# Output weights multiplied into the values, a last softmax by halves, and a new order of folding, in a four-layer kernel on one Trainium2 core

## The chip, the cores and the metric

One core of one Trainium2 chip runs the whole program. The metric is device time in microseconds (us). Runs of one kernel are compared by their fast state. Time before the change: 3512.23 us, the median of 3 runs (3511.39 to 3512.83).

## The reference, cut to what matters

The network has four layers. The change is in layer 0, a deformable attention over 2 samples of 512 channels and 32x32 pixels with 8 heads. Heads are handled two at a time, so there are 8 "pairs" (4 of each sample), with 1024 queries and 64 keys per head. What is costly is not the attention but its position bias: a small network with 128 hidden units runs for each query and key.

```
off  = tanh(pointwise(gelu(depthwise(q)))) * 4        # where the keys are sampled
kv   = grid_sample(xn, grid + off)
k, v = kw @ kv, vw @ kv                               # per head
pos  = grid_q[:, None] - grid_kv[None, :]
bias = relu(relu(signlog(pos) @ cpb_w1 + b1) @ cpb_w2 + b2) @ cpb_w3 + b3
attn = softmax(q k^T / 8 + bias)
out  = out_w @ concat_heads(attn @ v) + out_b         # <- the order of these two products changes
x    = x + out ;  x = x + mlp(bn2(x))
```

Some weights of layer 2 are multiplied together once, early in layer 0 ("folding"); its result does not depend on the data.

## The kernel before

The bias of all 8 pairs takes 256 steps of four points each. VectorE writes a point's first hidden layer, `h1`, into a ring of buffers; TensorE (PE) multiplies it (`z`), ScalarE applies the relu (`h`), VectorE and small DMA transfers join the parts of two steps ("joins"), and every 8 steps `third` multiplies the joined parts into the scores `sim`. The work for the next pair and the softmax of the last one run "behind", a piece per half step.

```python
ring = [one.tile([P, HW], F32, name=f"h1{k}") for k in range(4)]            # 4 buffers of its own
ring += [qkv2...[:, k * HW : (k + 1) * HW] for k in range(6)]               # 8 that lie where later
ring += [proj2...[:, k * HW : (k + 1) * HW] for k in range(2)]              # the MLP weights go (wa)
...
AHEAD = 8                                                                   # h1 is written 8 points ahead
for i in range(steps + 2):
    if i == steps:
        (w1s,) = load_w(wa, "wa", [a["mlp_w1"]])                            # 4 MB
        pps.append(zt([P, HW], "pp"))
        project_out(pps[0], 1, range(NPAIR - 2), oTs[B - 1])
    for k, part in enumerate((1, 0, 3, 2)):
        p = 4 * i + AHEAD + k
        if p < 4 * steps:
            h1s[p] = first(p)                                               # ring[p % len(ring)]
        if i < steps:
            parts.setdefault(i, {})[part] = second(i, four, part)           # z, then relu
        ...
        if i >= 3 and i % 2 and k == 0 and i < steps:
            nc.sync.dma_start(out=joins[i - 3][1:P:2], in_=joins[i - 2][0:P:2])
        if i >= 3 and i % 2 and k == 3 and i < steps:
            nc.gpsimd.dma_start(out=joins[i - 3][1:P:2], in_=joins.pop(i - 2)[1:P:2], accum_op=ALU.add)
        ...
```

The end of a pair, before (cut to the last pair's path):

```python
simb = two.tile(...); nc.scalar.activation(simb, sim, AF.Identity, bias=simbias[t])
pt = zt([P, 8, P], "pt")                        # 8 transposes of simb
nc.vector.tensor_reduce(mx, ptv, ..., ALU.max)  # then 16 exponentials, sums, division
pa = pt if last else zt([P, 8, P], "pa")        # 8 transposes back
nc.scalar.copy(aT, pa...)
pv = ...
for half in range(2):
    nc.tensor.matmul(pv[:, n], vbd[t], aT[:, n], start=True, stop=True)     # values
    if last:
        nc.scalar.copy(oT[:, pr, n], pv[:, n])
...
project_out(pp, m, ...)                         # 4 blocks: out_w on oT of the 4 pairs, then added to x
```

`zt` hands out in turn three buffers of 1024 columns in PSUM, to which this kernel's products are written and which `z`, `pt`, `pp`, `pb` and the rest share.

## Time and profile before

| stretch (us from the start) | what | length | PE busy |
|---|---|---|---|
| 0 to 62 | loads, offsets of pair 0, folding | 62 | 56.6 |
| 62 to 2009 | 256 bias steps | 1947 | 1940.8 |
| 2009 to 2063 | end of the last pair (the tail) | 54 | 42.9 |
| 2063 to 3510 | MLP and layers 1 to 3, untouched | 1447 | |

In this trace the granted clock is 0.50 or 0.51 in four stretches of the first 2063 us: for 3.4 us from 10.9 and from 2038.4, for 6.8 us from 38.2 and from 2018.0. 3.4 us of half clock are called a window below, so the longer stretches are two each; what starts one is not shown. In PE's rows, `128*32` (as for `z`) and `128*128` tell two forms of product apart; the prediction calls the form a mode. From the issue of the 4 MB load at 2004.77 to 2018.80 the DMA moved 299 GB/s.

The prediction further on shows the rows this table is cut from. Two more views of the kernel before are used later. The first is the chain of waits in the folding (start, length, what ran): small products `po`, `row` and `pb` (here the kernel's tile `pb2`, not the `pb` of the loop, which comes up later) stand together, and the folding's own products `pf` after them.

```profile
36.26 0.38 PE po L371 x2
36.64 1.00 PE row L715 x8
37.64 2.56 PE pb L135 x16
40.20 6.02 PE pf L135 x8
```

The second is the timeline of DMA issues just before the last `z` ends at 2009.39:

```profile
2004.77 2.31 SPq L119 DMA_DIRECT2D wa<-in_mlp_w  x4
2005.56 0.86 POOL L784 DMA_DIRECT2D h<-h  x1 [5.73 <-DVE h L543]
2007.04 0.83 POOL L780 DMA_DIRECT2D h<-h  x1 [0.61 <-DMA h<-h]
```

The 4 MB load of the MLP weights (`wa`) is issued 2.3 us ahead of the last join, the POOL line at 2007.04. Which edit of the change alters that order turns out to be the question of this study.

### The profile page before, as it was taken

How to read it: one execution, taken by the hardware profiler on the slowest of the kernel's cores; microseconds unless marked ns; L12 is line 12 of the kernel's file. 1: busy time of each engine (PE TensorE's matmuls, PEld its weight loads, DVE VectorE, ACT ScalarE, POOL GpSimd, SP SyncE). 2: the span in 40 equal slices, each digit the busy share in tenths (PEclk: the TensorE clock that was granted, in tenths of full speed). 3: DMA queues.
4: the chain of work that ended last, by engine and by line, in shares of the span. 5: the costliest groups of instructions: out<-in, count | busy, mean ns of one | idle time of the engine just before them, and what ended most of it. 6: DMA issues, size and time to landing. Idle time of an engine off the chain costs nothing.

```text
span 3510.3 us, 58708 instructions
## 1 busy us (share of the span) xinstructions
PE 3470.8 (99%) x24269; PEld 1452.0 (41%) x24269; DVE 2474.9 (71%) x2724; ACT 1761.3 (50%) x2478; POOL 494.2 (14%) x581
## 2 busy tenths in 40 slices
PE   9999999999999999999999999999999999999999
PEld 4333333333333333333333269999433333444443
DVE  6999999999996999999999835455264374130223
ACT  4867867867864868768776611112243242111110
POOL 0222222222221222222222200000001000000000
PEclk9999999999999999999999999999999999999999
DMA  5776676666674676666766710001100000000000
GB/s 171 149 150 145 130 152 142 143 146 136 145 150 88 144 149 134 142 145 136 149 144 145 163 64 12 13 10 57 35 1 1 1 0 0 15 0 0 6 30 25
DMA packets 133683, 313.38 MB, mean 89 GB/s; under 512 B 21088, under 2 KB 66528, under 8 KB 132640
## 3 DMA queue, kind: packets, MB, share of 16 engines
q0 software_dynamic: 57040, 200.31, 30.7%
q1 hardware_dynamic: 76224, 108.71, 9.1%
q8 instruction: 193, 3.16, 0.4%
q14 instruction: 82, 0.67, 0.1%
q10 hardware_dynamic: 144, 0.52, 0.0%
HBM read 64.12 MB, written 10.75 MB: 21 GB/s over the span
## 4 chain that ended last, share of the span: by engine, by line
PE 90%; DVE 6%; ACT 2%; issue 2%; DVEq 0%; POOL 0%; ACTq 0%; POOLq 0%
PE z L529 43%; PE pw L135 6%; PE pm L1266 5%; PE pma L135 5%; PE pmv L135 5%; PE pmb L135 4%; PE score L1377 4%; PE score L135 3%; PE pv L1425 3%; DVE wa L512 2%; PE sim L556 2%; DVE h L543 2%; PE ppr L1297 2%; PE pmp L135 2%; PE pp L637 1%
## 5 line engine op out<-in xcount | busy, mean ns | idle before, releaser
L538 ACT ACTIVATE h<-z,b2h 128x1024 f32<-128x1024 f32 x1024 | 1134.8, 1115 | 520.1 <-PE z L529 504.7
L529 PE MATMUL z<-wa,cpb_w 128*32 128x512 f32 x10880 | 1196.6, 593 | 4.1 <-ACT h L538 4.1
L512 DVE CUSTOM_DVE_ANT_1 wa<-tab,tab 128x1024 f32<-128x1024 f32 x680 | 799.6, 1217 | 28.2 <-PE z L529 25.9
L529 PEld LDWEIGHTS z<-wa,cpb_w 128*32 128x32 f32 x10880 | 346.2, 110 | 807.2 <-issue 722.5
L543 DVE SCALAR_TENSOR_TENSOR h<-h,turn,h 128x1024 f32<-128x1024 f32 x512 | 653.9, 1277 | 13.5 <-ACT h L538 13.1
L529 PE MATMUL z<-h,cpb_w 128*32 128x512 f32 x5504 | 612.6, 593 | 2.1 <-ACT h L538 2.1
L512 DVE CUSTOM_DVE_ANT_1 h<-tab,tab 128x1024 f32<-128x1024 f32 x344 | 404.5, 1217 | 15.3 <-PE z L529 15.1
L784 POOL DMA_DIRECT2D h<-h x255 | 224.9, 882 | 1080.5 <-DVE h L543 703.2
L529 PEld LDWEIGHTS z<-h,cpb_w 128*32 128x32 f32 x5504 | 174.9, 110 | 410.2 <-issue 361.3
L1378 ACT ACTIVATE p<-score 128x1024 f32<-128x1024 f32 x144 | 139.5, 1021 | 184.8 <-PE score L1377 184.8
L135 PE MATMUL pw<-p,vT 128*128 128x512 f32 x512 | 221.8, 593 | 1.3 <-DVE y L1483 1.3
L1308 DVE TENSOR_TENSOR acc<-acc,p 128x2048 f32<-128x2048 f32 x56 | 128.8, 2300 | 105.1 <-ACT p L1378 57.8
L1161 ACT COPY p<-pma 128x128 f32<-128x128 f32 x70 | 18.6, 266 | 304.3 <-PE pma L135 304.3
L776 POOL DMA_DIRECT2D h<-h x127 | 108.3, 853 | 402.4 <-DMA h<-h 397.7
L1310 DVE TENSOR_TENSOR acc<-p 128x2048 f32<-128x2048 f32 x12 | 27.5, 2291 | 183.6 <-ACT p L1512 110.0
L135 PEld LDWEIGHTS pw<-p,vT 128*128 128x128 f32 x512 | 97.0, 190 | 122.6 <-issue 121.0
L1153 DVE TENSOR_TENSOR upper<-pma,p 128x256 f32<-128x256 f32 x70 | 29.6, 422 | 163.7 <-ACT p L1161 163.6
L780 POOL DMA_DIRECT2D h<-h x127 | 126.2, 993 | 50.2 <-DMA h<-h 42.6
L1068 POOL TENSOR_SCALAR hc<-x,sc,sh 128x1024 f32<-128x1024 f32 x16 | 28.1, 1767 | 704.6 <-DVE sh L1064 507.9
L1377 PE MATMUL score<-q,k 64*128 64x512 f32 x512 | 127.2, 615 | 0.0
L1266 PE MATMUL pm<-hc,wa 128*64 128x512 f32 x512 | 122.4, 603 | 0.0
L1425 PE MATMUL pv<-p,vT 128*64 128x512 f32 x512 | 121.4, 595 | 0.0
(309 smaller groups left out, 3263.1 us busy)
## 6 DMA issues: line engine op xcount, KB each, us to landing
h<-h POOLq DMA_DIRECT2D x255, 512.0 KB, 4.8
h<-h POOLq DMA_DIRECT2D x254, 256.0 KB, 4.8
tab<-slog_d SPq DMA_DIRECT2D x128, 256.0 KB, 6.0
h<-h SPq DMA_DIRECT2D x127, 256.0 KB, 2.3
wa<-in_qkv_w SPq DMA_DIRECT2D x8, 768.0 KB, 6.3
xt<-in_xt SPq DMA_DIRECT2D x8, 512.0 KB, 4.9
wa<-in_mlp_w SPq DMA_DIRECT2D x4, 1024.0 KB, 12.5
wb<-in_mlp_w SPq DMA_DIRECT2D x16, 256.0 KB, 5.4
```

What stands on the lines that cost most here:

```text
L135: nc.tensor.matmul(pm, w, m, start=(k == 0), stop=(k == len(pairs) - 1))
L512: nc.vector._custom_dve(TENSOR_ADD_SAT, out=h1.rearrange("p (y x) -> p y x", x=W), in0=tx[:, quad, point, :].unsqueeze(1).to_broadcast([P, ...
L529: nc.tensor.matmul(z[point * 32 : point * 32 + 32, n], cpb_w2[:, lo : lo + 32], h1s[point][:, n], start=True, stop=True,)
L538: nc.scalar.activation(h2, z, AF.Relu, bias=b2h[:, part : part + 1])
L543: nc.vector.scalar_tensor_tensor(h2, h2, turn[:, part // 2 : part // 2 + 1], parts.pop(part + 1), ALU.mult, ALU.add)
L780: nc.gpsimd.dma_start(out=joins[i - 3][1:P:2], in_=joins.pop(i - 2)[1:P:2], accum_op=ALU.add)
L784: nc.gpsimd.dma_start(out=joins[i - 1], in_=other, accum_op=ALU.add)
L1266: nc.tensor.matmul(pm[at : at + wide], w[:, k, lo + at : lo + at + wide], h[k][:, n], start=(k == 0), stop=(k == CC - 1),)
L1308: nc.vector.tensor_add(acc, acc, p)
L1377: nc.tensor.matmul(sc[:, part, :], ks[part][r, left[part]], qs[part][r, n], start=True, stop=True)
L1378: nc.scalar.activation(p[:, :, n], sc, AF.Exp, scale=scale)
L1425: nc.tensor.matmul(pv[part * 64 : part * 64 + 64, n], vT[:, ls, lo : lo + 64], lp[:, part, n], start=(ls == 0), stop=(ls == 7),)
```

## The change

Its intent, in three parts. Part 1, folding: the small products are spread singly between folding blocks, so that PE does not run a stretch of tiny products. Part 2, values first: `out_w @ (attn @ v)` becomes `(out_w @ v) @ attn`; per pair a 128x512 product `pvo` replaces the 128x1024 product `pv`. The products `vo` of a sample's four pairs must be kept, and to make room one h1 buffer is given up (ring 12 to 11, lead 8 to 7). Part 3, the last pair: the softmax and projection by halves of the queries, and the last four steps multiplied singly ("fours") in place of being joined by DMA first; before, only the last two were. The 512 KB joins inside a step stay in both kernels; the last of them, for step 254, comes up again.

```diff
+        vop = l0.enter_context(tc.tile_pool(name="att_vo", bufs=NPAIR))
-        ring = [one.tile([P, HW], F32, name=f"h1{k}") for k in range(4)]
+        ring = [one.tile([P, HW], F32, name=f"h1{k}") for k in range(3)]
 ... (samples)
-            nc.tensor.matmul(pkv[:, 1, :], kv, bd["vw"][:, pr, :], start=True, stop=True)
+            nc.tensor.matmul(pkv[:, 1, :], bd["vw"][:, pr, :], kv, start=True, stop=True)
-            vbd[t] = two.tile([P, P], F32, name="vbd")
-            nc.scalar.copy(vbd[t], pkv[:, 1, :])
+            values = one.tile([P, P], F32, name="values")
+            nc.scalar.copy(values, pkv[:, 1, :])
             yield
+            pvo = zt([P, C], "pvo")
+            nc.tensor.matmul(pvo, values, ow, start=True, stop=True)
+            vos[t] = vop.tile([P, C], F32, name="vo")
+            nc.scalar.copy(vos[t], pvo)
             pb = zt([P, 1], "pb")
             nc.tensor.matmul(pb, kq, b1q[:, pr : pr + 1], start=True, stop=True)
             nc.vector.tensor_add(simbias[t], pb, col("cpb_b3"))
 ... (finish: pv, its copies and all "if last" cases go; the last pair has its own function)
+            for half, n in enumerate(halves):
+                third(sim, NR - 8, eights, fours, [half])
+                scores(t, sim, [half])
+                nc.scalar.activation(simb[:, n], sim[:, n], AF.Identity, bias=simbias[t])
 ... (transposes and maxima by halves; 6 products of pp beside the exponentials)
+            for half, n in enumerate(halves):
+                for m in range(3):
+                    project_out(pps[m], b, m, range(NPAIR) if m == 2 else [pr], [half])
+                    add_out(b, m, n, pps[m])
 ... (folding)
+        advance(steps)
+        advance(fold_steps)
         drain(steps)
-        advance(small_steps, 2)
+        advance(small_steps)
+        advance(fold_steps)
+        advance(small_steps)
 ... (loop)
-        AHEAD = 8
+        AHEAD = 7
+        (w1s,) = load_w(wa, "wa", [a["mlp_w1"]])
+        ends = [joins.pop(steps - 4 + j) for j in range(4)]
+        finish_last(sim, [joins.pop(steps - 8), joins.pop(steps - 6)], [ends[:2], ends[2:]])
```

## The prediction

> **What bounds it now.** First the page's engine line, then busy time by stage.
>
> ```profile
> PE 3470.8 (99%) x24269; PEld 1452.0 (41%) x24269; DVE 2474.9 (71%) x2724; ACT 1761.3 (50%) x2478; POOL 494.2 (14%) x581
> ```
>
> ```profile
> core 0: us, PE busy (x) PEld busy (x) DVE busy (x) ACT busy (x) POOL busy (x), PEclk, DMA share, GB/s
> 0.00:62.00 62.00, 56.56 (x209) 31.83 (x213) 40.50 (x108) 17.96 (x46) 4.87 (x17) 0.92 0.42 145
> 62.00:2009.00 1947.00, 1940.76 (x17378) 604.42 (x17370) 1845.81 (x1673) 1417.53 (x1906) 442.61 (x515) 1.00 0.67 143
> 2009.00:2063.00 54.00, 42.85 (x112) 17.58 (x108) 9.52 (x9) 9.35 (x38) 0.20 (x1) 0.91 0.24 76
> ```
>
> TensorE sets the time everywhere; the code after layer 0 (from 2063 us) is textually the same in both kernels. The change touches three stages: the folding (to 62 us), the 256 steps of the position bias (62 to 2009 us, PE busy 99.7%) and the tail of the last pair (2009 to 2063 us). In the loop only PE work or a new PE wait counts; in the other two, idle time and clock count too.
>
> The same busy-by-stretch view, on stretches that the clock records mark:
>
> ```profile
> 34.80:38.20 3.40, 2.35 (x21) 2.16 (x20) 2.88 (x19) 2.43 (x7) 0.00 (x0) 1.00 0.00 0
> 38.20:45.00 6.80, 6.80 (x17) 4.03 (x17) 5.58 (x11) 0.83 (x4) 0.00 (x0) 0.50 0.34 72
> 45.00:61.70 16.70, 16.70 (x55) 8.09 (x54) 13.77 (x14) 2.02 (x2) 0.00 (x0) 1.00 0.18 68
> 2017.90:2024.80 6.90, 4.71 (x14) 1.49 (x15) 0.00 (x0) 0.00 (x0) 0.00 (x0) 0.51 0.51 200
> ```
>
> After a stretch of tiny products (34.8 to 38.2) PE runs 6.8 us at half clock; so again after the tail's wait. Next, the chain of waits in the tail (start, length, what):
>
> ```profile
> 2009.39 3.63 PE pp L637 x8
> 2013.02 0.98 PE sim L556 x4
> 2014.00 6.09 issue
> 2020.09 5.99 PE sim L556 x16
> ...
> 2031.59 4.86 ACT at L590 x32
> ...
> 2045.25 17.27 PE pp L637 x40
> ```
>
> The 6.09 us called "issue" is a DMA wait. Between 2004 and 2024 us the DMA view has
>
> ```profile
> wa<-in_mlp_w SPq DMA_DIRECT2D x4, 1024.0 KB, 12.5
> h<-h POOLq DMA_DIRECT2D x1, 256.0 KB, 13.0
> ```
>
> The last 256 KB join was issued at 2007.04 and took 13.0 us instead of the page's median 4.8, because the MLP weights load beside it: 2007.04 + 13.0 = 2020.04, and PE goes on at 2020.09. Last, two timelines, around a value product of pair 1 and around its small product pb:
>
> ```profile
> 363.35 1.98 PE L615 MATMUL pv<-aT,vbd 128*128 128x512 f32 x4
> 365.26 3.64 PE L529 MATMUL z<-wa,cpb_w 128*32 128x512 f32 x32
> ```
>
> ```profile
> 478.81 0.38 PE L474 MATMUL pb<-b1q,kq 128*128 128x1 f32 x2
> ...
> 479.12 2.35 PE L529 MATMUL z<-wa,cpb_w 128*32 128x512 f32 x20
> ...
> 480.44 0.16 DVE L476 TENSOR_TENSOR simbias<-pb,pc 128x1 f32<-128x1 f32 x1
> ```
>
> Each f32 product has two records; one 128x512 product costs 0.86 us back to back (17.27 / 20). VectorE empties pb 1.3 us after PE wrote it; its queue runs behind.
>
> [...] pv is 1.72 us of work but takes 1.91 until the next z, and that run of z 3.57 instead of 3.43, together 2.05. [...]
>
> **Part 1, folding.** The removed costs: po waits 1.05 us for ScalarE; the next 8 pb products take 2.56 us at half clock, later ones 0.79 per 4, so 1.0 too much; 2 fold products (8 records) take 6.02 us instead of 3.54, so 2.5. Sum 4.5. Now a fold block stands before po, and pb products stand singly between blocks. Built up from the end of the third fold block at 34.10: 1.13 + 3.54 (fold 4) + 0.38 (po) + 1.0 (row) + 4 x 3.54 + 4 x 0.79 = 57.5, against 61.74. The fold's copy (1.0 us on ScalarE) fits under po and row. **-4.2 us.** The first table now comes about 3.2 us later (ScalarE's tanh waits behind that copy), so VectorE's fourth h1 ends near 54.5 instead of 51.3: still ahead of 57.5.
>
> **Part 2, loop.** Seven pairs lose pv: 7 x 2.05 = -14.3. Eight pairs gain pvo, one 128x512 product in a step that leaves the z mode anyway: 8 x 0.86 = +6.9. ScalarE's changes (oT copy 1.0 out, vo copy of half the width in) are not on the path. But the built order shows a new wait: pvo and pb now take two of the three PSUM buffers at once, and the very next z gets pb's buffer, waiting for simbias. Before, one z part (1.72 us) stood between. VectorE's place in its order shifts by half a step like PE's, so I keep its 1.3 us after pb's old end: pvo fills 0.86 of that, and the rest with the semaphore is a stall of about 0.65 us (simbias end 480.60 against a z that could start at 479.98). 8 x 0.65 = +5.2. Net **-2.2 us.**
>
> Ring 12 to 11 and AHEAD 8 to 7: a step's last h1 now stands at the head of the previous iteration on VectorE instead of before that iteration's join, and may start only when the step before has been read. So PE waits if VectorE starts an iteration over 6.87 - 1.2 = 5.6 us after PE starts that step. From the starts of h1 and z in the trace, this lag peaks at 5.0 in ordinary steps, and at 5.9 only in steps that last 7.9 us or more; the least reserve is 0.6. So 0, but thin.
>
> **Part 3, tail.** From the last z (E = 2009.35) to the last pp took 53.2 us. After, in E-relative us: 4 products of pp to 3.55; the last four steps are no longer joined by DMA but multiplied as fours (6 products in two concurrent sets, 1.72 per half), so third + scores of half 0 end at 6.3; the built program makes half 1 wait for half 0's copy (0.6), so to 9.7 for half 1; copy to 10.35; first transposes (0.55), their maximum on VectorE (0.68), and the second transposes wait for it: 11.6, maximum to 12.3. The 16 exponentials (4.86) to 17.2; PE fills this with 6 products (5.15, to 16.8). Transposes wait for all exponentials: 17.3 to 17.9; 2 products to 19.65; transposes to 20.25. Then no pv and no oT copy: pp of three blocks, two halves, 12 products, 10.3 to 30.55; block 3, 3.43 to 34.0, a wait for VectorE's addition (0.75), 3.43 to 38.2. **53.2 - 38.2 = -15.0 us**: of it 6.1 the DMA wait, about 4 the half clock, the rest pv and idle between. MLP weights now start at E, 4 MB at about 300 GB/s, 14 us: in time for E + 39.
>
> Sum: -4.2 - 2.2 - 15.0 = -21.4; 3512.2 - 21.4 = **3490.8**.
>
> **Rivals.** (a) VectorE takes over: it is 95% busy in the loop, and one buffer less makes PE wait near the end of each depthwise stretch. For it: the reserve of 0.6. Against: PE waits on it nowhere now. Some 1 to 2 us a pair would make 3500 to 3506. (b) The pb stall is larger, as VectorE may lag 2 to 3 us there: 1.5 us each would make 3497; with no stall 3485.5. (c) The clock halves anyway, in the folding because po and row stand together (+2.5), or in the tail among transposes and short waits (+1.7). (d) The join of step 254 lands late again beside the weights: it is issued about 3.6 us before E, so should land by E + 2, needed at E + 3.6.
>
> **Range and chances.** The three terms are sure in sign but the loop's sum runs from -7 to +5, tail and clock to about 3 more either way: 3483 to 3500. 2% is 70 us, more than the whole touched idle time (5.4 + 6.2 + 11.2 us) and the removed work together, so faster by over 2% is practically excluded, and slower would need over 10 us of new wait per pair.
>
> **What would show it.** Folding: full clock from 34 us, first z near 57.5. Loop: 8 waits of PE z on DVE simbias, 0.3 to 1 us each; step period still 6.87; no PE waits on h1. Tail: no gap over 1 us, last pp about 38 us after the last z, clock near 1.0. Wrong if PE waits on VectorE's h1 appear, if simbias waits exceed 10 us in all, or if the tail shows a half-clock window.

## The result, and the profile after

The changed kernel takes **3489.95 us** (median of 4 fast runs, 3488.45 to 3490.21) against 3512.28 us for the kernel before in the same rounds. The ratio is 0.9936 (95% interval 0.9919 to 0.9953). Ratios here are the mean time of one kernel's fast runs over that of the other's of the same rounds, so not quite the ratio of the medians quoted.

Busy time by stage of the changed kernel, same columns as in the prediction's table (start:end, length, then busy time and instructions of each engine, the granted PE clock, DMA):

```profile
0.00:57.50 57.50, 52.98 (x233) 30.27 (x237) 38.11 (x106) 19.32 (x47) 4.87 (x17) 1.00 0.46 166
57.50:1998.00 1940.50, 1928.70 (x17330) 602.70 (x17326) 1847.39 (x1675) 1410.85 (x1905) 440.97 (x513) 1.00 0.67 143
1998.00:2045.00 47.00, 42.68 (x151) 18.73 (x144) 15.48 (x24) 11.75 (x43) 2.37 (x5) 1.00 0.37 124
```

The clock is at 1.00 in all three; before it was 0.92 and 0.91 in the first and last. Exact marks from the two traces (a `z` row ends where the last `z` ends):

| mark to mark | before | after | difference | predicted |
|---|---|---|---|---|
| start to the first `pparts` product (before the folding differs) | 33.94 | 31.57 | -2.4 | 0 |
| `pparts` to first `z` (folding) | 27.73 | 23.26 | -4.5 | -4.2 |
| first `z` to the end of the last (loop) | 1947.72 | 1945.43 | -2.3 | -2.2 |
| from there to the end of the last `pp` (tail) | 53.11 | 38.99 | -14.1 | -15.0 |
| from there to the end | 1447.79 | 1448.84 | +1.1 | 0 |
| span | 3510.29 | 3488.09 | -22.2 | -21.4 |

The folding's chain of waits after the change, to be held against the one of before:

```profile
32.85 3.44 PE pf L135 x8
36.28 0.12 PE po L370 x2
36.40 1.00 PE row L754 x8
37.40 0.04 issue
37.44 3.70 PE pf L135 x8
```

A folding block now stands ahead of `po`, which waits no more, and the next one runs at full clock: 3.70 us for what took 6.02.

The tail's chain of waits after the change:

```profile
2000.27 3.63 PE pp L620 x8
2003.90 1.85 PE sim L562 x12
...
2013.27 4.85 ACT at L660 x32
...
2020.98 13.75 PE pp L620 x32
...
2034.75 0.76 DVE x L630
...
2035.56 3.71 PE pp L620 x8
```

`sim` follows `pp` at once; the 6.09 us of before are gone. And PE's waits (total us, times, longest us):

```profile
PE z L534 <- ACT h L543: 5.4, 11, 0.7
PE z L534 <- DVE simbias L481: 4.5, 8, 0.6
...
PE pk L135 <- issue: 1.7, 6, 0.7
```

The eight waits on `simbias` are new, as predicted. So are six short ones of `pk`, which the prediction did not have; `z`'s waits for ScalarE's `h` fell from 6.2 to 5.4 us. No wait for VectorE's h1 appears.

### The profile page after: what moved, and what is told of

The parts are those of the page before. It is cut to its first block, busy times and chain, and to the rows that moved or that the text cites. A ratio compares the mean times of both kernels' runs of the same rounds, so it can differ in the third digit from the quotient of the medians.

```text
span 3488.1 us, 58691 instructions
## 1 busy us (share of the span) xinstructions
PE 3452.3 (99%) x24257; PEld 1446.7 (41%) x24257; DVE 2477.1 (71%) x2731; ACT 1756.1 (50%) x2479; POOL 492.5 (14%) x579
## 4 chain that ended last, share of the span: by engine, by line
PE 77%; DVE 16%; issue 4%; ACT 2%; DMA 0%; DVEq 0%; SPq 0%; POOL 0%; ACTq 0%; POOLq 0%
PE z L534 32%; DVE wa L517 6%; PE pw L135 6%; PE pm L1306 5%; PE pma L135 5%; PE pmv L135 5%; DVE h L548 5%; PE pmb L135 4%; PE score L1417 4%; PE score L135 3%; PE pv L1465 3%; DVE h L517 2%; PE ppr L1337 2%; PE pmp L135 2%; PE pp L620 1%
## 5 line engine op out<-in xcount | busy, mean ns | idle before, releaser
L534 PE MATMUL z<-wa,cpb_w 128*32 128x512 f32 x11904 | 1779.1, 593 | 6.7 <-DVE simbias L481 3.4
L534 PE MATMUL z<-h,cpb_w 128*32 128x512 f32 x4480 | 986.3, 593 | 3.4 <-ACT h L543 2.2
L517 DVE CUSTOM_DVE_ANT_1 wa<-tab,tab 128x1024 f32<-128x1024 f32 x744 | 878.5, 1216 | 34.0 <-PE z L534 33.9
L534 PEld LDWEIGHTS z<-wa,cpb_w 128*32 128x32 f32 x11904 | 493.0, 110 | 883.6 <-issue 803.6
L534 PEld LDWEIGHTS z<-h,cpb_w 128*32 128x32 f32 x4480 | 256.3, 110 | 334.4 <-issue 291.3
L517 DVE CUSTOM_DVE_ANT_1 h<-tab,tab 128x1024 f32<-128x1024 f32 x280 | 333.1, 1217 | 11.4 <-PE z L534 11.2
```

Of the source, the lines that this page charges most:

```text
L517: nc.vector._custom_dve(TENSOR_ADD_SAT, out=h1.rearrange("p (y x) -> p y x", x=W), in0=tx[:, quad, point, :].unsqueeze(1).to_broadcast([P, ...
L534: nc.tensor.matmul(z[point * 32 : point * 32 + 32, n], cpb_w2[:, lo : lo + 32], h1s[point][:, n], start=True, stop=True,)
```

## The experiments

Three theories were to be told apart. **T1** (the prediction): each part brings its predicted share, and the tail's gain comes from Part 3, which needs no DMA join at the end. **T2**: the tail's gain comes from something else, the order of the 4 MB load and the last join. **T3**: part of the measured difference is half-clock windows falling differently from run to run. The rounds of the experiments ran on three chips (11, 0 and 2); each ratio compares runs of the same rounds.

### The kernel before once more, unchanged

> The kernel before, unchanged, profiled a second time, to see what of a trace repeats. Theory A: the half-clock stretch near 11 us in the first profile of before [...] will be elsewhere or absent here, so the first z moves from 61.7 to as early as 59; the half clock after the tiny products (38 to 45 us there) and the two in the tail follow from the program and come back. Rival B: the start is fixed by the program, so the half-clock stretch near 11 us comes back and the first z stands at 61.7 within 0.3. Time: ratio 1.000 within 0.001 either way.

Measured: 3509.16 us (3506.74 to 3512.89, 12 runs), ratio 0.9999 (0.999 to 1.0007). The runs of one program spread over 6 us. Its trace has `pparts` at 32.55 where the first had 33.94, no half-clock stretch near 11 us where the first had one, and 10.2 us of half clock from 35.3 us where the first had 6.8 from 38.2. The first `z` stood at 61.9 all the same, as the folding lost what the start had won. So T3 holds for a few us: what a single trace shows of the start is not all the program's.

### The new folding order alone

```diff
 # kernel before
         advance(fold_steps, 3)
         drain(bias_steps)
+        advance(steps)
+        advance(fold_steps)
         drain(steps)
-        advance(small_steps, 2)
+        advance(small_steps)
+        advance(fold_steps)
+        advance(small_steps)
 ... (and the same swap in the loop that follows)
```

> The kernel before with the new order of the folding alone. Theory A: from the start of pparts to the first z 27.6 us become 23.1 (in the changed kernel it is 23.1), no half clock in that stretch, time 3512.3 - 4.4 = 3507.9 (ratio 0.9987). Rival B (all of the 6.8 us that the changed kernel has won by its first z comes from this order): 3505.5, ratio 0.9981. Rival C (the order only moves the wait, as VectorE's first table comes later): first z no earlier, ratio 1.000.

Measured: 3506.83 us (21 runs), ratio 0.999 (0.9984 to 0.9997), so about 3.5 us less, 1 to 5.6 within the interval, which holds theory A (0.9987) and neither rival B (0.9981) nor C (1.000). `pparts` to first `z` is 23.27 us, the changed kernel's value to 0.01.

### The changed kernel with the old folding order

The same lines, reversed.

> The changed kernel with the old order of the folding. Theory A: pparts to first z goes back from 23.1 to 27.6 us, with a half-clock stretch after the tiny products; time 3490 + 4.4 = 3494.4 (ratio to before 0.9949). Rival B: 3490 + 6.8 = 3496.8 (0.9956). Rival C: 3490 (0.9936).

Measured: 3497.18 us (5 runs, 3494.52 to 3498.05), ratio 0.996 (0.9946 to 0.9974). `pparts` to first `z` goes back to 27.74. Loop and tail stay (1945.22 and 38.99 us), so the parts do not lean on one another here. By time alone theory A (0.9949) and rival B (0.9956) both lie within the interval, and B is the nearer. But in this trace the 2.4 us before `pparts` came back as well (33.94), with a half-clock window from 11.0 us, and the edit does not reach that stretch. Over all traces of this study the folding shows a plain pattern:

| folding | traces | half-clock windows of 3.4 us in it | `pparts` to first `z` |
|---|---|---|---|
| old | 2 | 1 | 26.1 |
| old | 3 | 2 | 27.7 |
| old | 2 | 3 | 29.4 |
| new | 6 | 0 | 23.3 |

Each window costs 1.65 us, and by extrapolation the old order without any would take 26.1 - 1.65 = 24.4. So the new order is worth 1.1 us of its own (the `po` wait) and one to three windows, 2.8 to 6.1 us in all. The predicted 4.2 fits the two windows that its one trace happened to show.

### `pb` written beside `pvo`

In the changed kernel, `pvo` and `pb` take two of the three PSUM buffers at once. The timeline around pair 1 shows what follows:

```profile
467.83 1.13 PE L475 MATMUL pvo<-ow,values 128*128 128x512 f32 x2
...
468.80 0.28 PE L479 MATMUL pb<-b1q,kq 128*128 128x1 f32 x2
...
469.40 0.16 DVE L481 TENSOR_TENSOR simbias<-pb,pc 128x1 f32<-128x1 f32 x1
...
469.61 0.63 PE L534 MATMUL z<-h,cpb_w 128*32 128x512 f32 x3 [0.54 <-DVE simbias L481]
```

`z` wants `pb`'s buffer and starts only when VectorE has emptied it. `pvo` fills 512 of a buffer's 1024 columns, so `pb` can go into the other half (the "second bank" of the expectation):

```diff
 # changed kernel
-            pvo = zt([P, C], "pvo")
-            nc.tensor.matmul(pvo, values, ow, start=True, stop=True)
+            pvo = zt([P, HW], "pvo")
+            pb = pvo[:, C : C + 1]
+            nc.tensor.matmul(pvo[:, :C], values, ow, start=True, stop=True)
-            pb = zt([P, 1], "pb")
```

> The changed kernel with pb written into the second bank of pvo's buffer, so that one buffer less is taken and the next z waits for ScalarE only. Theory: the 8 waits of z on simbias (4.5 us in all) go, and nothing takes their place: 3490 - 4.5 = 3485.5 (ratio 0.9924). Rival: VectorE, which runs behind there, then stops PE later in the pair (at an h1 or at the z two parts on, which now waits for simbias), so that the time stays at 3489 to 3490 (0.9934 to 0.9937).

Measured: 3482.93 us (5 runs, 3482.03 to 3486.0), ratio 0.9924 (0.991 to 0.9937). The same place in its timeline:

```profile
469.18 0.28 PE L477 MATMUL pvo<-b1q,kq 128*128 128x1 f32 x2
469.38 0.63 PE L534 MATMUL z<-h,cpb_w 128*32 128x512 f32 x3
```

`z` follows at once; no wait on `simbias` is left. The loop is 5.1 us shorter (1940.32 against 1945.43), a little more than the 4.5 us of waits. The median falls by 7; 2.7 us of that are in the time after the first MLP product (1444.8 against 1447.5), where the changed kernel's trace has a half-clock window at 2904 us and this one has none, and where the half clock at the very end of the trace lasts 3.9 us against 1.8. So nothing shows these 2.7 us to be the edit's. This version beats both kernels.

### The weights' load held back

```diff
 # kernel before
             nc.scalar.activation(simb, sim, AF.Identity, bias=simbias[t])
+            if t == NT - 1:
+                gate = dram.tile([P, 64], F32, name="gate")
+                nc.sync.dma_start(out=gate, in_=simb[:, :64])
+                late_w1.extend(load_w(wa, "wa", [a["mlp_w1"]]))
 ... (and the load at i == steps goes)
```

> Kernel before, except that the 4 MB load of the MLP's first weights waits behind a small transfer that reads the last pair's scores, so it does not run beside the last 256 KB join. Theory (the 6.09 us gap is the join slowed by that load, and the half clock after it follows from the gap): the join lands about 4.8 us after its issue instead of 13.0, the gap shrinks to under 1 us, the half-clock stretch after it vanishes (2.35 us), so about 8 us less: 3502 to 3504, ratio 0.9977. Last z to last pp 53.2 to about 45 us. Rival (the gap is the program's own, the additions of the last steps or a queue's order): gap and time unchanged within 1 us, or a later stall on the weights gives back what was won (first product of the MLP then waits).

Measured: 3499.0 us (7 runs, 3498.48 to 3504.48), ratio 0.9974 (0.9963 to 0.9985). The wait of `sim` is gone, so the theory of the DMA holds; the size was low. From the end of the last `z` to the first MLP product (`pmp` in the views) it takes 43.35 us in place of 54.53, so 11.2 less: 6.1 of the wait, and the other 5.1 go with the half clock, since not only the stretch after the wait (2018.0, two windows) but also the one at 2038.4 vanished. With the old values, the old softmax and all joins in place, one transfer's moment is worth over three quarters of the whole tail's gain of 14.2.

### The values first, alone

The kernel before with Part 2 (ring 11, lead 7 with it), but the old tail and the old folding.

> Kernel before with the values multiplied by the output weights first (buffers 11, lead 7), old tail, old folding order. Theory: loop 2.3 us shorter (7 pv less, 8 pvo more, 8 waits of z on simbias of 0.56 us), tail about 3 us shorter (no pv and no copy of its result), gap of 6 us for the last join still there: 3505, ratio 0.9985. Rival (the tail's gain of 14 us comes mostly from the values, not from halves and the missing joins): 3495 to 3498.

Measured: 3492.97 us (5 runs, 3492.23 to 3494.93), ratio 0.9957 (0.9943 to 0.997). The expectation missed by 12 us, and its rival's 3495 to 3498 was not low enough either. T1 falls as to the tail: the 6-us wait is gone although every DMA join is still there. Loop 1945.3 us, the changed kernel's 1945.4; from the last `z` to the first MLP product 40.62 us, where the changed kernel takes 40.31. **All of Part 3 is worth 0.3 us here.** In these tails PE idles 4.3 us with Part 3 and 5.3 without (windows view), but it is also busy 0.7 us longer, 36.0 against 35.3. The times cannot show so little: this run and the changed kernel with the old folding, which differ by Part 3 alone, have ratios of 0.9957 and 0.996, well within each other's intervals. Against 43.35 us with 11 buffers and the old values (the run of the shorter ring further on), Part 2's own removal of `pv` is worth 43.35 - 40.62 = 2.7 us. What took the wait away had to be in the other lines of this edit, and the one that moves a DMA is the ring.

Why the ring does so can be worked out from the code. There are 1024 h1, and the last step reads numbers 1020 to 1023. In a ring of 12 these are slots 0 to 3, the four tiles of its own; the last h1 that lies in the weights' place is number 1019, so the load is free to start a step before the end. (It was issued 4.6 us before the end of the last `z`, right behind a join of 2004.20 in the same queue; with Part 3 and 12 buffers, where there is no such join, it was 6.8 us before it.) In a ring of 11 they are slots 8, 9, 10 and 0, three of them in the weights' place, and the load has to wait for the last `z`: with the shorter ring alone it was issued at 2008.46, 0.1 us after the last `z` ended.

### Twelve buffers given back, with and without Part 3

To make room, `values` is written into a tile that is dead by then. Both kernels have the same edit, the one on the run of values alone, the other on the changed kernel:

```diff
-        ring = [one.tile([P, HW], F32, name=f"h1{k}") for k in range(3)]
+        ring = [one.tile([P, HW], F32, name=f"h1{k}") for k in range(4)]
-            values = one.tile([P, P], F32, name="values")
+            values = shift
-        AHEAD = 7
+        AHEAD = 8
```

> The run values_only with its 12th h1 buffer and lead of 8 given back (the values written into a tile that is dead by then, to make room). Of 12 buffers the four of the last step are not all its own, of 11 they cannot be: with 12, the last h1 in the weights' place is read a step before the end, so the 4 MB load may start 4.6 us before the last z, ahead of the last join; with 11 it starts with the last z, behind the join. Theory (the shorter ring, not the values and not the halves, took the DMA wait away): the gap of some 6 us before the third layer's products and the half clock after it come back, last z to first product of the MLP 52 instead of 40.6 us, time 3504. Rival (taking out pv and its order did it): stays at 3493.

Measured: 3506.09 us (21 runs, 3499.33 to 3507.79), ratio 0.9985 (0.9978 to 0.9991). The wait is back in the waits view,

```profile
PE sim L561 <- issue: 6.4, 1, 6.4
```

and so are 10.2 us of half clock; 50.99 us from the last `z` to the first MLP product. Its 21 runs also show T3 in one kernel: eleven with a mean granted clock of 0.996 average 3506.8 us, nine with 0.998 average 3501.0.

> The changed kernel with 12 h1 buffers and lead 8 (values in a dead tile). Theory, the prediction's step: the four last steps need no DMA join after the load starts, so the early load harms nothing: tail and time as the changed kernel, 3490, first MLP product 40.3 us after the last z. Rival (d) of the prediction: the join inside step 254 (issued 3.8 us before the last z) now falls behind a load that starts 4.6 us before it, lands some 13 us after its issue instead of 5, and is needed 3.6 us after the last z: a gap of about 5 to 6 us and perhaps a half-clock stretch, time 3496 to 3501.

Measured: 3494.98 us (5 runs, 3493.07 to 3498.1), ratio 0.9961 (0.9947 to 0.9975). The prediction's rival (d) comes true as soon as the ring has 12 buffers, with a shorter gap than the 5 to 6 us expected. The chain of waits:

```profile
1998.50 11.76 DMA h<-h
2010.25 0.04 issue
2010.30 3.62 PE sim L562 x6
```

The load is issued at 1995.51, the 512 KB join inside step 254 at 1998.50; it lands after 11.76 us and PE waits 3.4 us for it, and two windows run at half clock. From the last `z` to the first MLP product it takes 47.37 us. So Part 3 does shield the tail against an early load, by 51.0 - 47.4 = 3.6 us, but not wholly; and with 11 buffers there is no early load to be shielded from.

### Nothing but the shorter ring

```diff
 # kernel before
-        ring = [one.tile([P, HW], F32, name=f"h1{k}") for k in range(4)]
+        ring = [one.tile([P, HW], F32, name=f"h1{k}") for k in range(3)]
-        AHEAD = 8
+        AHEAD = 7
```

> Kernel before with nothing but 11 h1 buffers instead of 12 and a lead of 7 instead of 8. Theory (one buffer less lets the 4 MB load start only with the last z, behind the last join): no gap before the third layer's products, no half clock after it, last z to first MLP product 43.4 us as with the load held back, instead of 54.5; loop unchanged within 1 us; 3499 us, ratio 0.997. Rival (a buffer less costs PE waits on h1 and the gap belongs to the old tail): 3509 or more.

Measured: 3501.04 us (7 runs, 3496.02 to 3502.01), ratio 0.9971 (0.9959 to 0.9982). The DMA issues have changed places, against the first timeline of this document:

```profile
2006.03 0.83 POOL L780 DMA_DIRECT2D h<-h  x1 [0.59 <-DMA h<-h]
2008.46 1.05 SPq L119 DMA_DIRECT2D wa<-in_mlp_w  x2
```

No wait is left, no half clock in the tail, and from the last `z` to the first MLP product it takes 43.35 us: to 0.01 us what holding the load back gave. Two very different edits that both put the join ahead of the load give the same tail, which settles it: with the load held back there are 12 buffers and a lead of 8, so for the tail neither number matters but through the load. The loop is as before (1947.59 against 1947.72).

The tail, from the last `z` to the first MLP product, in one table:

| values, last softmax | 12 buffers | 11 buffers | difference |
|---|---|---|---|
| old, old | 54.5 | 43.4 | -11.2 |
| first, old | 51.0 | 40.6 | -10.4 |
| first, by halves | 47.4 | 40.3 | -7.1 |

So what each edit is worth depends on the order in which they are counted: the shorter ring 11.2 us when it comes first and 7.1 when it comes last, the halves 3.6 us with 12 buffers and 0.3 with 11.

### One buffer less still

```diff
 # changed kernel
-        ring = [one.tile([P, HW], F32, name=f"h1{k}") for k in range(3)]
+        ring = [one.tile([P, HW], F32, name=f"h1{k}") for k in range(2)]
-        AHEAD = 7
+        AHEAD = 6
```

> Changed kernel with one h1 buffer less (10 instead of 11) and a lead of 6 instead of 7: the rival of the prediction that VectorE's reserve is thin. By the lags in the trace of the changed kernel (at most 5.9 us near the end of a depthwise stretch, limit falls from 5.7 to about 4.5) PE should wait for h1 some 0.5 to 1.4 us in one or two steps of each depthwise stretch: loop 4 to 10 us longer, 3494 to 3500, waits of PE z on DVE h1 in the waits view. If the reserve is larger than the lags say: loop unchanged, 3490 as now. If it was already used up at 7: much more, over 15 us.

Measured: 3490.7 us (5 runs, 3487.97 to 3490.84), ratio 0.9945 (0.9931 to 0.9958); no wait for h1 in the view, and a loop 0.8 us longer. The expectation of 4 to 10 us missed. Worked out from the traces, the time from the end of a step's last h1 to the start of that step's products is the better measure. The changed kernel has at least 0.7 us of it in every step but one (step 147, 0.3 us), and 1.8 or more outside the first dozen steps and steps 145 to 147; one buffer less takes 1.2 us, one h1. Only the steps 146 and 148 grew by more than 0.1 us, by 0.9 us together. In most steps rival (a) was more than one buffer away, not a fraction of one; the lag between VectorE's and PE's starts, which the prediction used, overstated the danger.

### The changed kernel once more

> The changed kernel once more, unchanged, to see how far its runs spread and beside the run before it on one chip: 3486 to 3492, ratio 0.994; last z to first MLP product 40.3 us in any run. If the time of the first run was luck of the clock's windows, the median moves by over 3 us.

Measured: 3489.91 us (5 runs, 3488.03 to 3490.67), ratio 0.994 (0.9927 to 0.9954), last `z` to first MLP product 40.30 us, `pparts` to first `z` 23.27. The result is not a lucky run, and these two marks are within 0.01 us of the first trace's.

## Why the prediction was right, point by point

**The sum.** 3490.8 predicted, 3489.95 measured, 0.9 us off. The stage terms fell within 1 us of the trace each. The remaining differences, -2.4 us before the folding and +1.1 us after the tail, are places that the change does not reach; that they cancel in part is luck. The first `pf` product starts at 21.2 to 22.3 us in the seven traces of this study without a half-clock window before 15 us and at 22.7 to 23.5 in the six with one, among both the old and the new folding orders; the first trace of the kernel before has one, that of the changed kernel none. After the tail it is the changed kernel's trace that has one more, at 2904 us.

**Folding** (-4.2 predicted, -4.5 in the first pair of traces): right, with each of its three terms visible, no `po` wait, full clock for `row`, `pb` and the next `pf`. (Its "2 fold products (8 records)" are four, at two records each; the sum does not depend on it.) But the step read two half-clock windows from one trace as if they belonged to the program. They fall one to three at a time, so the part is worth 2.8 to 6.1 us; that the measured pair of traces met the predicted size is luck.

**Loop** (-2.2 predicted, -2.3): right. The stall of `z` on `simbias` was predicted as 8 x 0.65 = 5.2 us and came as 8 waits of 0.56, 4.5 us. Its cause, the PSUM buffer shared in turn, is shown by the run that moved `pb`. The new `pk` waits (1.7 us) were not foreseen, and part of why the sum still held is that they offset the smaller stall and the 0.8 us less of waits for `h`. They stand in every run that has Part 2 and in none that has not, the run of the shorter ring alone included, so they come with the values; what in Part 2 causes them stays open.

**Tail** (-15.0 predicted, -14.1): right in size, and wrong about what earns it. The walk through the new tail was sound and ended at 38.2 us, measured 38.99: the scores of half 0 ended at 6.55 in place of 6.3, the exponentials at 17.85 in place of 17.2, and the rest stayed within 0.8. The failed step is the placing of the 6.1 us DMA wait, and of the half clock behind it, under Part 3, where the last four steps "are no longer joined by DMA". The runs show instead that, counted in this order, 11.2 of the 14.2 us to the first MLP product come from the ring's twelfth buffer, given up for space in Part 2; 2.7 come from `pv`; 0.3 from Part 3. So the size came out right by luck: with 12 buffers, Part 3 leaves a wait of 3.4 us and two windows at half clock. The prediction had both halves of this in hand. It noted that the weights now start at the last `z`, and it named in rival (d) a join that lands late beside them. It costed the shorter ring as 0 since it asked only what a buffer less does to the loop, and did not ask what it does to the transfer that waits for the buffer's place. Nor did it walk the old tail with the new transfer order, which would have shown that little is left for the halves.

A small transfer took longer when it was issued behind the large one: 256 KB take 13.0 us when issued 2.3 us after the 4 MB load, 512 KB take 11.8 us when issued 3.0 us after it in the changed kernel with 12 buffers, and joins of either size on the same queue (POOL's) take 4.8 us in the median of the profile page of the kernel before. Issued 2.4 us ahead of the load, as with the shorter ring alone, the join lands after 5.2 us and makes nobody wait. How the two transfers share the DMA engines is not shown.

**Clock.** The tail and folding ran at full clock (1.00 granted), as predicted, in all traces of the changed kernel and of every kernel with its folding and ring. The prediction counted the half clock in the tail as about 4 us; 5.1 were saved with the wait.

**Rivals.** (a) did not occur, and a further buffer less cost 0.8 us. (b) did not occur: the stall was 0.56 us, less than the 0.65 of the main estimate. (c) did not occur. (d) did not occur with 11 buffers (the join landed 1.8 us after the last `z`), and did with 12 (7.9 us after it).

## What to carry to other kernels

A buffer that borrows another tensor's place also sets when that tensor's load may start (here one buffer less moved it by 4.7 us): when a ring's length changes, work out which slots the last items use and what transfer that releases, early or late. When several edits land together and the sum comes out right, undo them one at a time before crediting any of them; here two changed numbers, the ring's length and the lead, gave half of the whole gain, and the largest piece of new code next to nothing. Where a tiny product takes a whole PSUM buffer out of a short rotation, an unused half of another buffer can be the cheap way out: here it took 5.1 us off the loop.

## Figures measured on the way

- The clock: in the old folding, 3.4 us of short products, 2.35 of them busy in the first trace and with no idle moment over 1.05 us, were followed by one, two or three windows at half clock, 1.65 us lost each, from trace to trace (two and three in the two traces of one kernel). The runs of one kernel spread by up to 8.5 us of 3510, and go with the granted clock (0.996 and 0.998: 3506.8 and 3501.0 us on average).
- A small transfer beside a large one: joins of 256 and 512 KB on POOL's queue took 4.8 us in the usual traffic of the loop; 512 KB took 11.8 us and 256 KB 13.0 us behind a 4 MB load, and 256 KB issued 1.5 to 2.4 us ahead of it landed after 4.7 to 5.2 us.
- A product between products of another form: `pv` (`128*128`), 1.72 us of work between runs of `z` (`128*32`), took 2.05, so 0.33 us for both changes of form. No run tested the form as the cause.
- A ring of buffers in another tensor's place: one buffer less moved that tensor's load by 4.7 us against the last `z`, and the first MLP product by 11.2.
